# Quarter slots for short last tiles of experts, and columns of A moved on chip, in a graph layer followed by a mixture of experts

## The chip, the cores and the metric

One core of a Trainium2 chip runs the whole program. The engines have instruction streams of their own: TensorE (PE, with its weight loads shown as PEld), VectorE (DVE), ScalarE (ACT), GpSimd (POOL) and SyncE (SP), which issues most DMAs. The metric is the device time of one launch in microseconds. Everything is float32 unless said otherwise.

## The reference

```python
edge_index = jnp.stack([src, dst])                       # 67584 edges, sorted by dst
x = x + gnn(layernorm(x), edge_weight, edge_index, node_vec1)
x = x + moe_ffn(layernorm(x)[None], Wr, br, ln_g, ln_b, W1, b1, W2, b2)[0]

# gnn:  segment_sum(w[:, None] * xn[dst], src, 2048) + node_vec1
# moe:  logits = xt @ Wr + br; the best 2 of 8 experts; weights renormalised
#       xn = layernorm(xt); xe = xn * ln_g[e] + ln_b[e]
#       y = gelu(xe @ W1[e] + b1[e], exact) @ W2[e] + b2[e]
```

x is 2048 x 256; an expert has 256 inputs and 1024 hidden units. So 4096 (token, expert) rows are computed. With the reference's own inputs the eight experts get 544, 509, 506, 482, 502, 510, 536 and 507 rows (counted by running the reference's routing).

## The kernel before

**Graph stage.** The sparse sum is made dense: A (2048 x 2048) is built in 32 steps of 64 columns (`for n in range(NH)`), two steps to a block `cb` of 128 columns. In step n DVE and POOL make the one-hots `hl` and `hr` of step n+1 (`make_hots`, three buffers each, lines 306 to 318). PE multiplies them in `make_cols` (line 343): 96 bf16 products with a stationary operand of 32 columns, at four column positions of the array by turns (`tile_position=(0, j * RK)`), each 128 wide. ACT copies each half of the result to `ar` (line 346; three buffers). The row of `ar` is (column in a group of four, block of A's rows), which is not how PE needs it, so SP writes `ar` to DRAM (`ad`, line 347) and, once a block's two steps are there, loads it back with a column of A to each partition (`ac`, line 350). `dense` (line 357) then multiplies, for two blocks of output rows, the `ac` tiles of a group of three or four blocks by `xn_sb`, the normalised x with 8 router columns (264 wide); `add` (lines 364 to 369) adds that to `acc` on DVE. These 40 pieces of work (`todo`) are dealt out by a budget: from step 8 on each step earns 3.5, a piece of a group costs its number of blocks (3 or 4), and the last step runs what is left of all groups but the last. On PE a step's pieces come after its `make_cols`, and PE works strictly in that order. Tiles `ac` come from two pools of four buffers, used by the groups in turn; a block of group g takes a buffer of group g-2. `xn_sb` is written by ACT in steps 0 to 3 (line 519), its router columns by DVE in step 5 (line 515). If some edge fell outside the windows, a branch after the stage does the sum another way; it isn't taken here.

**Expert stage.** Rows are routed on chip. A whole slot has 256 rows of one expert, a half slot 128. `run_slot` does the first layer (`layer_1`, line 1013: 8 chunks of the hidden units, two 256-wide products of two instructions each, the gelu on ACT at line 1015), the turning and scaling of the next slot's rows (`head`, lines 978 to 1002), and the second layer (`layer_2`, line 1027, twice for a whole slot), after which POOL adds rows to `y_d` in DRAM by index (`put_y`, line 1035). PE's order is written out by hand (`manual_schedule`). `slots` (lines 858 to 909) counts on DVE each expert's tiles: `n_of[:, 0]` whole slots and `n_of[:, 1]` a half slot for an odd tile; from it come the expert numbers `slot_i`, read into registers of SP (line 1134), and the row lists. The third expert's rows (`whole[3]`) are the first that need these. Ten whole slots always run (`FIRST = 10`, of which the loop at line 1151 runs u = 3 to 9); more run under nested conditions (line 1162), then the halves (line 1169), and at the end two whole slots (`final`) whose results are written to `out` after `y_d` has been copied there (line 1180). Weights and rows of the first two half slots are loaded in u = 4 and 5, and half 0's `head` runs in u = 8.

With the counts above, 34 tiles of 128 rows are needed: 16 whole slots (10, then 4, then the 2 at the end) and 2 half slots.

Of the kernel before, what the change touches and what calls it, by code (L numbers as in the profile page):

```python
# [9 lines left out]
F32 = mybir.dt.float32  # L10
BF16 = mybir.dt.bfloat16
F16 = mybir.dt.float16
I32 = mybir.dt.int32
# [13 lines left out]
def kernel(  # L27
# [57 lines left out]

    consts = ctx.enter_context(tc.tile_pool(name="consts", bufs=1))
# [60 lines left out]
    slot_i = consts.tile([1, NU + 2], I32, name="slot_i")  # L147
    xr_d = dram.tile([N + TS, RW], F32, name="xr_d")
    y_d = dram.tile([N + TS, D], F32, name="y_d")
    cols_d = dram.tile([NE, P, KH + 2 * KD], F32, name="cols_d")  # L150
# [178 lines left out]
    def make_cols(n, hl, hr):  # L329


        cb, h = n // 2, n % 2
        if h == 0:
            ads[cb] = dram.tile([P, NB, P], F32, name="ad", bufs=4)
        ad_v = ads[cb].rearrange("(m j) b r -> (j b) m r", m=GB // QP)
        ar = rowsp.tile([P, GH // QP, P], F32, name="ar")
        for m0 in range(0, GH // QP, 4):
            pa = ps_a.tile([P, 4, P], F32, name="pa")
            for m in range(4):
                for i in range(3):  # L340
                    for j in range(QP):
                        g = (m0 + m) * QP + j
                        nc.tensor.matmul(pa[j * RK:(j + 1) * RK, m, :], hr[:, i, g, :],  # L343
                                         hl[:, g, :], start=(i == 0), stop=(i == 2),
                                         tile_position=(0, j * RK))
            nc.scalar.copy(ar[:, m0:m0 + 4, :], pa)  # L346
        nc.sync.dma_start(ad_v[:, h * GH // QP:(h + 1) * GH // QP, :], ar)
        if h == 1:
            acs[cb] = pool_of[cb].tile([P, NB, P], F32, name="ac")
            nc.sync.dma_start(acs[cb], ads[cb])  # L350
# [20 lines left out]
    ads, acs = {}, {}  # L371
    ET = mybir.EngineType
    ALL = {ET.DVE, ET.Pool, ET.PE, ET.Activation, ET.SP}
    with tc.manual_schedule(engines=ALL):
# [88 lines left out]
        for n in range(NH):  # L463
# [36 lines left out]
            if n >= 8:  # L500
                budget += 3.5
# [8 lines left out]
            if n < 2:  # L510
                weigh_x(2 + n)
            elif n == 2:
                nc.scalar.copy(acc[:, :, D:], xl.rearrange("p (b e) -> p b e", e=NE))
            elif n == 5:
                nc.vector.tensor_tensor(xn_sb[:, :, D:], acc[:, :, D:],
                                        rs[:, :, None].to_broadcast([P, NB, NE]), OP.mult)
            if n < 4:
                for b in range(4 * n, 4 * n + 4):
                    nc.scalar.activation(xn_sb[:, b, :D], acc[:, b, :D], AF.Identity,
                                         bias=shift[:, b:b + 1], scale=rs[:, b:b + 1])  # L520
            if n == 1:
# [47 lines left out]
    with tc.If(n_used < E):  # L569
        nc.sync.dma_start(xn_d.rearrange("(b p) d -> p b d", p=P), xn_sb)  # L570
# [72 lines left out]
    class Slot:  # L643


        def __init__(self, i, n, set_, to, head_, early=False):
# [5 lines left out]

    LAST = 2
# [4 lines left out]
             for i, k in enumerate(numbers)]  # L658
    final = [Slot(FIRST - EARLY, TT, 3, AHEAD + 2, 2), Slot(FIRST - EARLY + 1, TT, 6, AHEAD + 6, 0)]
    halves = [Slot(NF + i, 1, 4 + i if i < 2 else i % 3, AHEAD + 3 + i % 3, 3 + i % 2)  # L660
              for i in range(NE)]
    with tc.manual_schedule(engines=ALL - {ET.Pool}):
# [195 lines left out]
        def slots(ps):  # L858


            small_t = lambda name, dt=F32: route.tile([P, NE], dt, name=name, bufs=1)
            flag = flags[:, 1:1 + NE]
            tiles_i = small_t("tiles_i", I32)
            nc.vector.tensor_tensor(tiles_i, ps, over, OP.add)
            nc.vector.tensor_scalar(tiles_i, tiles_i, 7, None, op0=OP.arith_shift_right)
# [9 lines left out]
                                           op1=OP.subtract)  # L875
            upto = route.tile([P, 2, NE], F32, name="upto", bufs=1)
# [20 lines left out]
            nc.vector.tensor_copy(slot_i[:, NU:], upto[0:1, :, NE - 1])  # L897
# [69 lines left out]
        def load_slot(s):  # L967
            load_weights(s)
            load_rows(s)
# [89 lines left out]
        def run_slot(s, nxt, more=(), between={}, put=put_y):  # L1059
            for m in more:  # L1060
                m()
            hT = layer_1(s)
            if nxt is not None:
                head(nxt)
            layer_2(s, hT, put, between)

        def later(load, *slots):
            return [lambda s=s: load(s) for s in slots]
# [68 lines left out]
        )  # L1137
        load_slot(whole[EARLY])
# [10 lines left out]
        for t in so_far:  # L1149
            nc.vector.memset(t, 0.0)  # L1150
        for u in range(3, FIRST):
            more = later(load_slot if u + 2 <= FIRST else load_rows, whole[u + 2])
            more += later(load_slot, *{4: halves[:1], 5: halves[1:2], 7: final[:1], 8: final[1:]}.get(u, []))
            also = {FIRST - 2: halves[0], FIRST - 1: final[0]}.get(u)
            run_slot(whole[u], whole[u + 1], more, {1: lambda: head(also)} if also else {})
# [3 lines left out]
    )  # L1159
    with ExitStack() as nest:  # L1160
# [6 lines left out]
    with ExitStack() as nest:  # L1167
        for u, s in enumerate(halves):
            nest.enter_context(tc.If(n_half > s.i - NF))
            with tc.manual_schedule(engines=ALL - {ET.Pool}):  # L1170
                if u >= 2:
                    head(s)
                run_slot(s, halves[1] if u == 0 else None,
                         later(load_slot, *halves[u + 1:u + 2] * (u > 0)))
# [38 lines left out]
```

## Time and profile before

| what | us |
|---|---|
| three timed runs | 505.18, 511.9, 511.95 (median 511.9) |
| the profiled execution | 508.05 |
| its span, first to last instruction | 506.3 |
| mean granted TensorE clock | 0.945 of full |

In the profile, a line like `PE L343 MATMUL pa<-hl,hr ... x96` is a run of 96 instructions of line 343, with its start and length; a bracket after it gives the engine's idle time before it and what ended that. The chain of waits follows the work that ended last backwards; an entry there is a start, a length and what took it.

### The profile page before, as it was taken

How to read it: one execution, taken by the hardware profiler on the slowest of the kernel's cores; microseconds unless marked ns; L12 is line 12 of the kernel's file. 1: busy time of each engine (PE TensorE's matmuls, PEld its weight loads, DVE VectorE, ACT ScalarE, POOL GpSimd, SP SyncE). 2: the span in 40 equal slices, each digit the busy share in tenths (PEclk: the TensorE clock that was granted, in tenths of full speed). 3: DMA queues.
4: the chain of work that ended last, by engine and by line, in shares of the span. 5: the costliest groups of instructions: out<-in, count | busy, mean ns of one | idle time of the engine just before them, and what ended most of it. 6: DMA issues, size and time to landing. Idle time of an engine off the chain costs nothing.

```text
span 506.3 us, 12113 instructions
## 1 busy us (share of the span) xinstructions
PE 459.8 (91%) x4996; PEld 394.4 (78%) x4996; DVE 273.1 (54%) x621; ACT 183.8 (36%) x422; POOL 192.7 (38%) x158
## 2 busy tenths in 40 slices
PE   4876599898979999899999899999999999999993
PEld 3775478687758878788888788888888888888882
DVE  7999999999969971317837232323232312212111
ACT  2478524144214210028483323332243433333320
POOL 3477655544533330000142444443452444322231
PEclk9575679899979999999999999999999999999998
DMA  6128678796777667953513997997999677226420
GB/s 214 53 76 246 203 223 269 230 236 186 203 216 221 210 178 239 344 189 105 179 54 84 303 333 214 361 356 210 334 360 309 169 210 210 36 40 204 140 92 31
DMA packets 84356, 102.15 MB, mean 202 GB/s; under 512 B 8240, under 2 KB 74656, under 8 KB 82176
## 3 DMA queue, kind: packets, MB, share of 16 engines
q1 hardware_dynamic: 74832, 86.26, 53.5%
q0 software_dynamic: 7984, 13.91, 11.9%
q10 hardware_dynamic: 1472, 1.06, 0.7%
q8 instruction: 44, 0.72, 0.6%
q14 instruction: 24, 0.20, 0.1%
HBM read 75.18 MB, written 28.14 MB: 204 GB/s over the span
## 4 chain that ended last, share of the span: by engine, by line
PE 35%; DMA 13%; issue 3%; DVE 1%; SPq 0%; ACT 0%; POOL 0%; POOLq 0%; DVEq 0%
PE py L1027 16%; PE ph L1013 15%; DMA xs<-xr_d,to_i 8%; DMA y_d<-ys,to_i 2%; DMA out<-y_d 2%; PE px L978 1%; PE px L834 1%; PE py L357 1%; DMA so_far<-out,to_i 1%; DMA out<-ys,to_i 0%; SPq L1180 0%; POOL out L1048 0%; POOLq L1209 0%; ACT L1015 0%; DVE pick L957 0%
## 5 line engine op out<-in xcount | busy, mean ns | idle before, releaser
L357 PE MATMUL py<-xn_sb,ac 128*128 128x264 f32 x512 | 126.3, 404 | 1.8 <-DVEq L569 1.4
L1013 PE MATMUL ph<-xeT,w 128*128 128x256 f32 (+1 forms) x576 | 121.3, 368 | 2.4 <-PEq L1167 1.7
L1027 PE MATMUL py<-w,hT 128*128 128x256 f32 x544 | 121.0, 379 | 0.0
L1013 PEld LDWEIGHTS ph<-xeT,w 128*128 128x128 f32 x576 | 104.4, 190 | 16.5 <-issue 3.0
L357 PEld LDWEIGHTS py<-xn_sb,ac 128*128 128x128 f32 x512 | 98.5, 197 | 21.7 <-issue 2.2
L1027 PEld LDWEIGHTS py<-w,hT 128*128 128x128 f32 x544 | 101.9, 190 | 12.9
L1015 ACT ACTIVATE hT<-ph,ec 128x256 f32<-128x256 f32 (+1 forms) x144 | 66.2, 462 | 117.6 <-PE ph L1013 60.8
L1035 POOL DMA_INDIRECT y_d<-ys,to_i x30 | 48.5, 1616 | 119.3 <-DVE ys L1030 88.5
L318 POOL TENSOR_TENSOR hr<-eq,w 128x1024 bf16<-128x1024 bf16 x32 | 61.2, 1912 | 81.6 <-DVE hr L318 66.1
L343 PE MATMUL pa<-hl,hr 128*32 128x128 bf16 x3072 | 58.4, 237 | 21.6 <-POOL hr L318 10.8
L343 PEld LDWEIGHTS <-hr 128*32 128x32 bf16 x3072 | 50.0, 106 | 32.6 <-issue 14.0
L306 DVE TENSOR_TENSOR hl<-k,iota_t 128x4096 bf16<-128x4096 bf16 x32 | 72.9, 2278 | 0.0
L987 DVE TENSOR_SCALAR xeT<-px,ec 128x256 f32<-128x256 f32 (+1 forms) x38 | 18.4, 526 | 79.8 <-PE px L978 79.0
L939 POOL DMA_INDIRECT xs<-xr_d,to_i x39 | 40.5, 1038 | 54.2 <-DVE z L702 41.9
L346 ACT COPY ar<-pa 128x512 f32<-128x512 f32 x64 | 36.5, 584 | 59.8 <-PE pa L343 53.6
L1030 DVE SCALAR_TENSOR_TENSOR ys<-py,wt,b2w 128x256 f32<-128x256 f32 x34 | 16.4, 484 | 72.7 <-PE py L1027 61.3
L364 DVE TENSOR_TENSOR acc<-acc,py 128x528 f32<-128x528 f32 x32 | 22.3, 701 | 35.3 <-PE py L357 35.3
L318 DVE TENSOR_TENSOR hr<-eq,w 128x2048 bf16<-128x2048 bf16 x32 | 39.1, 1223 | 0.6
L1002 ACT ACTIVATE b2w<-b,wt 128x256 f32<-128x256 f32 x36 | 16.3, 500 | 34.0 <-DVE wt L1000 32.4
L311 DVE TENSOR_TENSOR eq<-k,iota_t 128x1024 bf16<-128x1024 bf16 x32 | 21.8, 680 | 0.0
L670 ACT ACTIVATE sq<-acc,less_m 128x256 f32<-128x256 f32 x16 | 8.0, 499 | 32.6 <-DVE acc L364 32.6
L296 ACT CAST w<-r 128x256 bf16<-128x256 f32 x16 | 6.5, 405 | 25.0 <-DVE r L295 25.0
(196 smaller groups left out, 303.0 us busy)
## 6 DMA issues: line engine op xcount, KB each, us to landing
w<-in_L_ffn_W SPq DMA_DIRECT2D x40, 1024.0 KB, 9.2
ad<-ar SPq DMA_DIRECT2D x32, 512.0 KB, 8.7
ac<-ad SPq DMA_DIRECT2D x16, 1024.0 KB, 5.9
b<-in_L_ffn_b SPq DMA_DIRECT2D x20, 128.0 KB, 9.8
out<-y_d SPq DMA_DIRECT2D x4, 512.0 KB, 6.3
xr_d<-rec SPq DMA_DIRECT2D x1, 1300.0 KB
y_d<-acc SPq DMA_DIRECT2D x1, 1280.0 KB, 5.1
acc<-in_x SPq DMA_DIRECT2D x2, 512.0 KB, 7.6
```

What stands on the lines that cost most here:

```text
L306: nc.vector.tensor_tensor(hl.rearrange("p g (n t) -> p g n t", t=2), two(k2[:, 0], g, P), pair(P), OP.is_equal)
L311: nc.vector.tensor_tensor(eq.rearrange("p g (n t) -> p g n t", t=2), two(k2[:, 1], g, RK), pair(RK), OP.is_equal)
L318: return engine.tensor_tensor(hr[:, i0:i1].rearrange("p i g (n t) -> p (i g) n t", t=2), eq[:, None, :, :].to_broadcast([P, i1 - i0, GH, RK]),
L343: nc.tensor.matmul(pa[j * RK:(j + 1) * RK, m, :], hr[:, i, g, :], hl[:, g, :], start=(i == 0), stop=(i == 2), tile_position=(0, j * RK))
L346: nc.scalar.copy(ar[:, m0:m0 + 4, :], pa)
L357: nc.tensor.matmul(pa[:, i, :DX], acs[c][:, b + i, :], xn_sb[:, c, :], start=(c == cbs[0]), stop=(c == cbs[-1]))
L364: nc.vector.tensor_add(acc[:, b:b + 2, :], acc[:, b:b + 2, :], pa[:, :, :DX])
L939: nc.gpsimd.indirect_dma_start(out=(sets[s.set][0] if into is None else into)[:, t, :], out_offset=None, in_=(xr_d if rows is None else ro ...
L1013: nc.tensor.matmul(ph, w1[:, k, c * P:(c + 1) * P], xeT[:, k, :], start=(k == 0), stop=(k == KD - 1))
L1015: nc.scalar.activation(hT[:, c, :s.n * P], ph, AF.Gelu, bias=ec[:, c:c + 1], scale=1.0)
L1027: nc.tensor.matmul(py, hT[:, c, t * P:(t + 1) * P], w2[:, c, :], start=(c == 0), stop=(c == KH - 1))
L1035: st = nc.gpsimd.indirect_dma_start(out=y_d[:, :], out_offset=bass.IndirectOffsetOnAxis(ap=tos[s.to][:, t:t + 1], axis=0), in_=ys, in_offs ...
```

## The change

**Columns of A.** `ar` no longer goes through DRAM. As soon as ACT has copied half of a step's result, four DMAs of 64 KB move its four 128 x 128 pieces straight to `ac`, each to eight partitions that are four apart; of a step's eight, six are issued by SP and two by ACT. So `ac` is allocated at a block's first step. The columns of a block now stand in another order in the partitions, so `xn_sb` has to be permuted likewise: at the end of step 3 four DMAs write it to DRAM (`xn_p`) in permuted rows, and in step 5 one DMA reads all of it back in place. Its router columns are therefore written in step 3, and pieces of `dense` begin in step 7.

**Quarter slots.** An expert whose odd tile has 1 to 32 rows gets a quarter slot in place of a half slot, for at most two experts (`NQ`). `slots` finds them (`few_e`, `few_t`) and takes them out of the halves. Both quarter slots always run, spread over u = 7 to 9: the rows are the stationary operand (32 columns), four products at four column positions make the hidden units as 32 rows x 4 x 256, which are turned by two transposes, and the second layer leaves four partial sums that one product with `fold` adds up. The halves come ahead of the conditional whole slots, and load their data when they run.

```diff
+    xn_p = dram.tile([P, NB * DX], F32, name="xn_p")
+    xp = xn_p.rearrange("(q j m) f -> q m j f", m=4, j=8)
...
         if h == 0:
-            ads[cb] = dram.tile([P, NB, P], F32, name="ad", bufs=4)
-        ad_v = ads[cb].rearrange("(m j) b r -> (j b) m r", m=GB // QP)
+            acs[cb] = pool_of[cb].tile([P, NB, P], F32, name="ac")
...
             nc.scalar.copy(ar[:, m0:m0 + 4, :], pa)
-        nc.sync.dma_start(ad_v[:, h * GH // QP:(h + 1) * GH // QP, :], ar)
-        if h == 1:
-            acs[cb] = pool_of[cb].tile([P, NB, P], F32, name="ac")
-            nc.sync.dma_start(acs[cb], ads[cb])
+            for m in range(m0, m0 + 4):
+                c = h * P // 2 + m0 * QP * GC + m % 4
+                queue = nc.sync if m < 6 else nc.scalar
+                queue.dma_start(acs[cb][c:c + 4 * QP * GC - 3:4], ar[:, m, :])
...
-            if n >= 8:
+            if n >= 7:
                 budget += 3.5
...
-            elif n == 5:
+            elif n == 3:
                 nc.vector.tensor_tensor(xn_sb[:, :, D:], acc[:, :, D:],
                                         rs[:, :, None].to_broadcast([P, NB, NE]), OP.mult)
+            elif n == 5:
+                nc.sync.dma_start(xn_sb.rearrange("p b d -> p (b d)"), xn_p)
...
+            if n == 3:
+                for i in range(4):
+                    nc.sync.dma_start(xp[i], xn_sb[32 * i:32 * (i + 1)])
...
+            few_i = small_t("few_i", I32)
+            nc.vector.tensor_scalar(few_i, tiles_i, QR.bit_length() - 1, None,
+                                    op0=OP.arith_shift_right)
+            nc.vector.tensor_scalar(few_i, few_i, TS // QR - 1, None, op0=OP.bitwise_and)
...
+            nc.vector.tensor_scalar(is_few, few_i, float(P // QR), None, op0=OP.is_equal)
+            n_few = small_t("n_few")
+            nc.vector.tensor_tensor_scan(n_few, ones[:, :NE], is_few, 0.0, op0=OP.mult, op1=OP.add)
+            last = small_t("last")
+            nc.vector.scalar_tensor_tensor(last, iota_p[:, :NE], float(NB), tiles[:, :NE],
+                                           op0=OP.mult, op1=OP.add)
+            for i in range(NQ):
+                it = small_t(f"few{i}")
+                nc.vector.scalar_tensor_tensor(it, n_few, float(i + 1), is_few, op0=OP.is_equal,
+                                               op1=OP.mult)
+                nc.vector.tensor_sub(n_of[:, 1, :], n_of[:, 1, :], it)
+                of_it = small_t(f"of_few{i}")
+                for t, v in ((few_e, iota_p[:, :NE]), (few_t, last)):
+                    nc.vector.scalar_tensor_tensor(of_it, it, 1.0, v, op0=OP.mult, op1=OP.mult,
+                                                   accum_out=t[:, i:i + 1])
+            nc.vector.tensor_scalar(few_t, few_t, -1.0, None, op0=OP.add)
+            nc.vector.tensor_copy(slot_i[:, NU + 2:], few_e[0:1, :])
...
+            def first():
+                ph = ps_h.tile([P, TS], F32, name="ph")
+                for k in range(KD):
+                    for j in range(QW):
+                        nc.tensor.matmul(ph[part(j), :], xeT[:, k, :],
+                                         w1[:, k, j * TS:(j + 1) * TS], start=(k == 0),
+                                         stop=(k == KD - 1), tile_position=(0, j * QR))
+                nc.vector.tensor_copy(hs, ph)
...
+            def second():
+                pa = listed.rearrange("p a b -> p (a b)")
+                for t in range(TT):
+                    for j in range(QW):
+                        nc.tensor.matmul(pa[part(j), :], hT[:, t, part(j)], w2[:, j * TT + t, :],
+                                         start=(t == 0), stop=(t == TT - 1),
+                                         tile_position=(0, j * QR))
+                nc.vector.tensor_copy(py, pa)
+
+            def total():
+                pa = counts.rearrange("p a b e -> p (a b e)")[:QR, :D]
+                nc.tensor.matmul(pa, fold, py, start=True, stop=True)
...
+            if 0 <= f - 1 < NQ:
+                between_1 = {1: ready[1], 5: ready[2]}
+                between[0] = ready[3]
+                between.setdefault(1, lambda: None)
+                t0, t1 = between[1], ready[4]
+                between[1] = lambda t0=t0, t1=t1: (t1(), t0())
```

Here f is u - 7; `between_1` names the chunks of a whole slot's first layer ahead of which a step of the quarter slot stands (the products of `first` ahead of chunk 1, the transposes of `turn_h` ahead of chunk 5), and `between` the halves of its second layer ahead of which `second` (0) and `total` (1) stand.

## The prediction

> **What bounds the kernel now.** I read the page's busy slices first, then busy time by stage (cut where PE's lines change), then the chain of waits, and the timeline around what the change touches. Busy tenths in 40 slices of 12.7 us:
>
> ```profile
> PE   4876599898979999899999899999999999999993
> DVE  7999999999969971317837232323232312212111
> ```
>
> DVE fills the first third, PE everything after. The stages (columns: PE, PEld, DVE, ACT, POOL busy, granted clock, DMA share, GB/s):
>
> ```profile
> 66.30:191.70 125.40, 116.10 (x2542) 93.99 (x2534) 112.14 (x142) 39.26 (x91) 55.49 (x35) 0.95 0.75 218
> 191.70:238.50 46.80, 45.28 (x222) 38.13 (x211) 16.34 (x37) 13.48 (x41) 0.52 (x3) 1.00 0.68 226
> 238.50:452.40 213.90, 211.86 (x1041) 185.84 (x1039) 74.90 (x295) 79.72 (x169) 83.15 (x65) 1.00 0.73 222
> 452.40:469.20 16.80, 14.59 (x99) 13.38 (x99) 3.26 (x12) 6.39 (x17) 4.32 (x4) 1.00 0.63 167
> 469.20:506.30 37.10, 28.30 (x132) 24.64 (x132) 4.68 (x11) 8.48 (x18) 9.69 (x9) 0.94 0.28 90
> ```
>
> From the first `dense` (66.3) to the last `make_cols` (191.7) PE idles 9.3 us of 125 and DVE 13.3: both bind by turns. Then PE alone binds. From 238.5 to 452.4 (whole slots) it idles 2.0 us; 452.4 to 469.2 is the two half slots; the last row is the two final slots and the writes. The chain agrees:
>
> ```profile
> 268.87 0.67 PE listed L813 x12
> ...
> 280.14 7.48 DMA xs<-xr_d,to_i
> 287.63 0.04 issue
> 287.67 0.44 PE px L978 x2
> ...
> 309.27 6.91 PE ph L1013 x32
> ```
>
> PE's one wait among the slots is at 287.67, for the third expert's rows, gathered after `slots`. 32 instructions of 256 columns take 6.91 us, 0.216 each. In the graph stage:
>
> ```profile
> 47.40 2.08 ACT L519 ACTIVATE xn_sb<-acc,shift,rs 128x256 f32<-128x256 f32 x4
> ...
> 108.94 1.52 PE L343 MATMUL pa<-hl,hr 128*32 128x128 bf16 x96
> 110.39 2.94 PE L357 MATMUL py<-xn_sb,ac 128*128 128x264 f32 x12
> ```
>
> `xn_sb` is complete at 49.5. The 96 products with 32 columns take 1.45 us up to the next line, 15 ns each; the 12 full ones of L813, of the same 128 columns and width of data, 56 ns each: four column positions overlap 3.7-fold in 16-bit.
>
> **Half slots out.** PE's 14.6 busy us of 452.4 to 469.2 go, and half 0's head (0.22). The 2.2 us of PE idle there stand at the two exits from nested conditions ("PEq L1160" 0.6, "PEq L1167" 1.7); two exits remain, one now after u = 9, so they stay. The end behind follows PE as before: the last scatter is now a whole slot's second, 0.9 us after that slot's PE work at 453.3, against 469.1 for the last half's with `final` starting at 469.2. Gain 14.8.
>
> **Quarter slots in.** PE executes, for each: `turn` 0.22 (as half a head), `first` and `second` 16 instructions of 256 columns each, `turn_h` 0.22, `total` 0.43. In series `first` is 16 x 0.216 = 3.46; at the 3.7-fold overlap 0.93. Bounds: 2 x 2.7 = 5.5 us and 2 x 7.8 = 15.6. A written f32 product is two instructions (the page counts 544 of L1027 for 272 written), and both go to the same 32 columns, so only the second of one can lie beside the first of the next: 2-fold, 1.9 with the ends. So 4.7 each, 9.4 in all. [...] The DVE copies, the bias and the gelu between these steps have three to four chunks of 0.86 us on PE as cover; DVE is 35% busy in this stage. If that cover fails, each quarter slot adds the 0.5 us of a copy. Loads are unchanged (two slots' weights in u = 4 and 5); POOL scatters two of 32 rows; `fold` is one small DVE instruction in u = 3, under the same cover.
>
> **More in `slots`.** 15 DVE instructions and four accumulator reads, at the 0.18 us from start to start of its 28 neighbours between 268.28 and 273.30, and 0.1: 3.1 us. Behind them on DVE stand the new row lists, the scaling of slot 2's rows and `ys`; for them waits POOL's gather, and for that PE at 287.67. It is later by all of it, as PE waits already: +3.1, at least 0 (if the gather's 7.5 us shrink) and at most 3.4 with two more register loads.
>
> Expert stage: -14.8 + 9.4 + 3.1 = -2.3, from -9.3 to +4.2.
>
> **Columns on chip.** Behind `ar` stood two DMAs:
>
> ```profile
> ad<-ar SPq DMA_DIRECT2D x32, 512.0 KB, 8.7
> ac<-ad SPq DMA_DIRECT2D x16, 1024.0 KB, 5.9
> ...
> y_d<-acc SPq DMA_DIRECT2D x1, 1280.0 KB, 5.1
> ```
>
> 48 become 256 of 64 KB. At 0.34 to 0.43 us of queue time per issue, SP's six cost 2.4 of a step's 5.4 us (125.4 over 23 steps; SP has little else there), ACT's two 0.8 of its 3.7 us idle. PE waited 0.4 us in all for `ac`, so the shorter path itself gives nothing. The router columns' product (0.28 us on DVE) only moves from step 5 to 3. ACT's DMAs can wait for an `ac` buffer; I walked the budget: block 7 (step 14) needs group 0 done, now at step 13; block 10 (step 20) waits one piece, 2.9 us; block 13 (step 26) until step 27, about 7 us with ACT's copies queued behind. Three PSUM buffers cover that, or nearly: 0 to 1.
>
> **One step earlier.** By the budget, 28 pieces instead of 26 are done before step 31, so two of the six behind it (72 instructions, 16.3 us with their adds) go from there: -5.9, PE alone binding. They must fit before, where PE idles 9.3 us, 6.6 of it "issue" stalls of which I can't say that they give way. I take half as absorbed: -3.
>
> **`xn_sb` through DRAM.** 2112 KB are written after 49.5, and read back only then: SP waits in between, with the columns of step 6 on queued behind it, and step 7's `dense` waits on PE with every later `make_cols` behind. At y_d's pace (1280 KB in 5.1 us) the write takes 8.4; reading at ac's pace (1024 KB in 5.9) at most 12.2, I take 9 as half of the 5.9 is not bytes. 49.5 + 0.8 of issue + 17.4 = 67.7 (range 62 to 71): first `dense` 1.4 us later than now, though one piece ahead, and DVE, three buffers ahead, runs on. I count this in the absorbed half. Graph stage: -3, from -5.9 to +2.
>
> [...]
>
> **The sum.** -2.3 - 3 = -5.3: span 501, execution 502.8 from the profiled 508.05. That lies 3.9 under the median 511.9 (runs 505.18 to 511.95), so I go up by a third of it: 504.
>
> **Rivals.** *The detour of `xn_sb` is the new wait* (slower). If the four writes keep a quarter of the engines busy, then at 343 GB/s for 0.98 of 16 engines (200 to 210 us), 21.9 KB/us each, 2.16 MB take 24.7 us, ready at 84. PE idles from about 63 and is 18 behind, DVE stops when its three buffers are full at about 74; the idle time behind recovers 6 or so. Graph stage +11, with -2.3: +9, 518. It decides from a write of about 14 us on. For it: 32 partitions a DMA, where every row above has 128. Against: four DMAs in flight at once. *No overlap in f32*: quarter slots 15.6, +0.9 in all, 510. For: the pairs of instructions. *Full overlap*: 5.5, and -5 in the graph stage: -11, 498. For: the 3.7-fold of L343. *The slots don't apply*: 544 rows leave exactly 32, the limit, and 536 leave 24; a row more and one half stays, +7.3, 511. The nearest routing choice is decided by 0.0003 of a logit, so unlikely.
>
> **Chances.** Forecast 0.36, full overlap 0.18, detour 0.33, no overlap 0.11, not applied 0.02. Range 496 to 519, 2 us past full overlap and 1 past the detour; some 0.2 lies outside. 2%, about what a measurement here can tell from no change, is 10 us. Faster by that: full overlap and a third of the forecast's spread, 0.3; slower: four fifths of the detour, 0.27; within, 0.43.
>
> **What would show it.** Right: first `dense` near 67, no PE gap there, 48 instructions of L357 behind step 31, `first` at about 1.9 us, rows of slot 3 some 3 us later after `slots`, no half slots after u = 13. Wrong: PE idle between 63 and 84 with the read of `xn_p` issued near 75 (detour); `first` near 3.5 or 0.95; ACT waiting for `ac` in other steps than 20 and 26, or column DMAs that land later than 5.4 us each step, which would make DMA the bound.

## The result, and the profile after

| kernel | median us | runs | ratio [95%] |
|---|---|---|---|
| before | 508.86 | 505.18 to 511.95, 4 runs | |
| changed | 543.4 | 542.05 to 546.87, 4 runs | 1.069 [1.058, 1.080] |

The change makes the kernel 34.5 us slower; the range forecast ended at 519. The profiled execution of the changed kernel took 546.87, its span is 544.8; that is 38.5 more than the span in the profile of before, and this execution is the slowest of the four. Busy tenths in 40 slices, now of 13.6 us each:

```profile
PE   4877510398999998798999989999999969999993
DVE  7986920099999999322485733222333321222111
```

PE and DVE stand still together in the sixth to eighth slice, some 35 us; before, DVE had no such hole. The time line of PE (start, length, engine and line, work; in brackets the idle time before it and what ended that) shows where:

```profile
66.92 2.75 PE L351 MATMUL pa<-hl,hr 128*32 128x128 bf16 x96 [2.63 <-ACT ar L354]
103.98 4.50 PE L367 MATMUL py<-xn_sb,ac 128*128 128x264 f32 x12 [34.30 <-DMA ac<-ar]
```

L367 is `dense`: its first instruction comes at 103.98, and came at 66.35 before. The releaser named, `ac<-ar`, is only the wait that ended last of several; SP's own time line shows what else stands ahead:

```profile
55.27 8.29 SPq L360 DMA_DIRECT2D ac<-ar  x8
63.67 5.30 SPq L536 DMA_DIRECT2D xn_p<-xn_sb  x4
69.07 24.65 SPq L360 DMA_DIRECT2D ac<-ar  x12
93.83 0.49 SPq L528 DMA_DIRECT2D xn_sb<-xn_p  x1
```

The four writes of `xn_sb` are issued from 63.67 on, then the twelve column DMAs of steps 4 and 5, which take SP 24.65 us in place of some 8, and only then the read. What the DMA engines did meanwhile (the first two rows of the DMA view for 64 to 104 us: mean busy tenths of the 16 engines and GB/s in 40 slices of 1 us):

```profile
DMA  5422543353224222222232212233335959999321
GB/s 158 165 101 84 167 134 123 129 202 137 104 104 151 109 104 96 112 104 121 106 136 122 70 53 85 58 85 102 96 98 159 309 221 407 424 373 407 128 78 49
```

From 66 to 94 two or three tenths of the engines are busy in most slices and some 110 GB/s move, the columns included; in the read, behind 94, it is up to nine tenths and about 400 GB/s. The write can be told from the columns by its packets, 128 of 16.9 KB: in the trace they run from 65.3 to 87.5, four at a time. Meanwhile the columns hardly move: of their 512-byte packets on SP's queue 3 start between 74 and 84. SP, which waits for earlier column transfers before it issues more, stands still for 32.2 us in all (its waits between 40 and 110 us: total, times, longest):

```profile
SPq L360 <- DMA ac<-ar: 32.2, 8, 9.9
```

So when the write has landed at 87.5, eight columns are still to be issued ahead of the read, which follows 6.3 us later.

The stages, in the columns of the table of before (from the last products ahead of the gap to the first `dense`; to the last `make_cols`; what is left of `dense`; row choosing and slots up to u = 9; the jump over the halves with what surrounds it; the two final slots):

```profile
66.90:104.00 37.10, 2.77 (x97) 2.53 (x96) 5.25 (x4) 4.25 (x12) 6.21 (x5) 0.55 0.43 150
104.00:234.70 130.70, 122.05 (x2654) 99.15 (x2654) 113.69 (x145) 39.44 (x92) 52.99 (x33) 0.97 0.40 110
234.70:276.90 42.20, 40.06 (x195) 33.70 (x188) 15.19 (x35) 13.55 (x42) 0.52 (x3) 1.00 0.64 213
276.90:435.00 158.10, 154.27 (x805) 131.14 (x805) 63.88 (x266) 60.41 (x128) 59.44 (x47) 1.00 0.77 240
435.00:452.00 17.00, 12.45 (x49) 9.47 (x49) 4.77 (x18) 2.76 (x6) 5.68 (x6) 0.90 0.62 168
507.00:544.80 37.80, 28.30 (x132) 24.63 (x132) 5.08 (x12) 8.50 (x18) 9.82 (x9) 0.95 0.30 90
```

From the first to the last `dense` the two kernels take the same: 172.4 us before (66.35 to 238.72, where the row choosing starts), 173.0 now (103.98 to 276.95). Only the cut between the second and third row moved: 130.7 and 42.2 us in place of 125.4 and 46.8, since fewer pieces are left for the end. The DMA share fell from 0.75 to 0.40, and that brought nothing. From the last `dense` to the end of the span it is 267.6 before and 267.9 now, although the half slots are gone. Two places in it answer for that. The quarter slots themselves are cheap, and a jump isn't (PE's time line, in u = 7 and at u = 10):

```profile
407.37 1.07 PE L1151 MATMUL ph<-w,xeT 128*32 128x256 f32 x16
408.37 3.72 PE L1056 MATMUL ph<-xeT,w 128*128 128x256 f32 x16
...
444.02 0.67 PE L1056 MATMUL ph<-xeT,w 128*128 128x256 f32 x2 [0.97 <-PEq L1312]
448.27 8.43 PE L1056 MATMUL ph<-xeT,w 128*128 128x256 f32 x30 [3.58 <-issue]
```

`first` (L1151) is 16 instructions in 1.00 us up to the next line, 62 ns each against 216 ns for one that uses all columns of the array: 3.5-fold overlap in f32 (216 / 62). But at the eleventh whole slot, where the code of eight half slots is jumped, PE loses 0.97 and 3.58 us and runs 30 instructions in 8.43 in place of 6.5: 6.5 us in all.

So the loss is one stretch of 37.6 us in the graph stage, which the stage behind doesn't give back, and a gain in the expert stage that another place takes away. The experiments ask whether the stretch is the trip of `xn_sb` through DRAM (theory 1) or the 256 column transfers (theory 2), and what each other part is worth.

### The profile page after: what moved, and what is told of

It reads as the page before. It is cut to its first block, busy times and chain, and to the rows that moved or that the text cites. A ratio compares the mean times of both kernels' runs of the same rounds, so it can differ in the third digit from the quotient of the medians.

```text
span 544.8 us, 12426 instructions
## 1 busy us (share of the span) xinstructions
PE 458.9 (84%) x4972; PEld 387.5 (71%) x4972; DVE 276.3 (51%) x643; ACT 178.8 (33%) x408; POOL 191.0 (35%) x157
## 5 line engine op out<-in xcount | busy, mean ns | idle before, releaser
L367 PE MATMUL py<-xn_sb,ac 128*128 128x264 f32 x512 | 123.7, 397 | 36.6 <-DMA ac<-ar 34.5
L367 PEld LDWEIGHTS py<-xn_sb,ac 128*128 128x128 f32 x512 | 96.1, 193 | 56.5 <-issue 37.4
L1056 PE MATMUL ph<-xeT,w 128*128 128x256 f32 x512 | 116.9, 385 | 5.6 <-issue 3.6
L1070 PE MATMUL py<-w,hT 128*128 128x256 f32 x512 | 114.3, 380 | 0.0
L1056 PEld LDWEIGHTS ph<-xeT,w 128*128 128x128 f32 x512 | 97.6, 192 | 21.6 <-issue 5.7
L1070 PEld LDWEIGHTS py<-w,hT 128*128 128x128 f32 x512 | 95.8, 190 | 13.1 <-issue 0.8
L1058 ACT ACTIVATE hT<-ph,ec 128x256 f32<-128x256 f32 x128 | 60.5, 474 | 110.1 <-PE ph L1056 59.2
L1078 POOL DMA_INDIRECT y_d<-ys,to_i x28 | 45.4, 1623 | 108.0 <-DVE ys L1073 73.8
L351 PE MATMUL pa<-hl,hr 128*32 128x128 bf16 x3072 | 62.0, 239 | 22.7 <-ACT ar L354 8.5
L351 PEld LDWEIGHTS <-hr 128*32 128x32 bf16 x3072 | 53.0, 106 | 34.6 <-issue 23.4
L982 POOL DMA_INDIRECT xs<-xr_d,to_i x36 | 37.6, 1044 | 57.7 <-DVE z L721 40.9
L1030 DVE TENSOR_SCALAR xeT<-px,ec 128x256 f32<-128x256 f32 x34 | 16.9, 539 | 75.1 <-PE px L1021 74.4
L377 DVE SCALAR_TENSOR_TENSOR acc<-py,cols,acc 128x256 f32<-128x256 f32 x16 | 7.0, 478 | 36.4 <-PE py L367 36.3
```

The costliest lines, as they stand in the source:

```text
L367: nc.tensor.matmul(pa[:, i, :DX], acs[c][:, b + i, :], xn_sb[:, c, :], start=(c == cbs[0]), stop=(c == cbs[-1]))
L982: nc.gpsimd.indirect_dma_start(out=(sets[s.set][0] if into is None else into)[:, t, :], out_offset=None, in_=(xr_d if rows is None else ro ...
L1056: nc.tensor.matmul(ph, w1[:, k, c * P:(c + 1) * P], xeT[:, k, :], start=(k == 0), stop=(k == KD - 1))
L1058: nc.scalar.activation(hT[:, c, :s.n * P], ph, AF.Gelu, bias=ec[:, c:c + 1], scale=1.0)
L1070: nc.tensor.matmul(py, hT[:, c, t * P:(t + 1) * P], w2[:, c, :], start=(c == 0), stop=(c == KH - 1))
L1078: st = nc.gpsimd.indirect_dma_start(out=y_d[:, :], out_offset=bass.IndirectOffsetOnAxis(ap=tos[s.to][:, t:t + 1], axis=0), in_=ys, in_offs ...
```

## The experiments

Each ratio is to runs of the kernel before on the same chip (medians 504.4 to 508.9); times in brackets are of kernels whose experts get other numbers of rows. "First" is the start of the first `dense`, "end" the start of the row choosing behind the last one, "rest" what is left of the span from there.

| run | median us | ratio [95%] | first | end | first to end | rest |
|---|---|---|---|---|---|---|
| before, profile shown | 508.86 | | 66.35 | 238.72 | 172.4 | 267.6 |
| before_again | 510.24, one run | | 66.89 | 242.29 | 175.4 | 266.2 |
| the change | 543.4 | 1.069 [1.058, 1.080] | 103.98 | 276.95 | 173.0 | 267.9 |
| change_again | 547.08, one run | | 103.19 | 276.96 | 173.8 | 268.0 |
| quarter_only | 508.98 | 1.006 [1.002, 1.011] | 66.84 | 242.82 | 176.0 | 262.2 |
| quarter_only_again | 510.4, one run | | 66.77 | 244.51 | 177.7 | 264.1 |
| quarter_halves_last | 517.79 | 1.026 [1.018, 1.033] | 68.09 | 244.08 | 176.0 | 272.1 |
| cols_only | 542.49, one run | | 102.73 | 274.47 | 171.7 | 266.2 |
| no_detour | (558.04) | | 69.19 | 242.93 | 173.7 | |
| straight_write | (571.87) | | 86.70 | 257.78 | 171.1 | |
| cols_neighbours | 566.28 | 1.117 [1.109, 1.125] | 77.52 | 302.64 | 225.1 | 263.0 |
| cols_neighbours_sp | 517.38 | 1.019 [1.009, 1.028] | 66.91 | 251.59 | 184.7 | 261.6 |
| moved_by_pe | 522.26 | 1.032 [1.027, 1.038] | 85.22 | 257.74 | 172.5 | 262.4 |
| moved_by_pe_71 | 528.05 | 1.043 [1.037, 1.049] | 83.42 | 263.65 | 180.2 | 262.9 |
| moved_by_pe_5ar | 539.1 | 1.067 [1.061, 1.073] | 83.85 | 273.64 | 189.8 | 262.7 |
| x_twice | 513.59 | 1.019 [1.014, 1.023] | 76.56 | 247.87 | 171.3 | 263.1 |
| before_7 | 507.5 | 1.007 [1.002, 1.012] | 61.61 | 237.81 | 176.2 | 267.9 |
| quarter_7 | 506.24 | 1.002 [0.998, 1.006] | 64.22 | 244.29 | 180.1 | 260.7 |

**The two halves of the change apart.** `cols_only` is the kernel before with the graph hunks of the diff, `quarter_only` the change without them:

```diff
-            for m in range(m0, m0 + 4):
-                c = h * P // 2 + m0 * QP * GC + m % 4
-                queue = nc.sync if m < 6 else nc.scalar
-                queue.dma_start(acs[cb][c:c + 4 * QP * GC - 3:4], ar[:, m, :])
+        nc.sync.dma_start(ad_v[:, h * GH // QP:(h + 1) * GH // QP, :], ar)
+        if h == 1:
+            acs[cb] = pool_of[cb].tile([P, NB, P], F32, name="ac")
+            nc.sync.dma_start(acs[cb], ads[cb])
...
-                for i in range(4):
-                    nc.sync.dma_start(xp[i], xn_sb[32 * i:32 * (i + 1)])
```

> The kernel before with the graph part of the change alone (columns moved on chip, xn_sb permuted through DRAM, pieces from step 7). Theory (the graph part makes the whole loss): first dense at 104 us, the last one ends at 277, 544 to 548 in all. Rival (graph and expert parts act on one another): an end of the last dense that differs from 277 by over 4 us.

> The change without its graph part: columns of A go through DRAM as before, pieces of dense begin in step 8, xn_sb is not permuted; the quarter slots and the halves ahead of the whole slots stay. Theory (the graph part makes the whole loss): first dense at 66 us and end of the last dense at 239, as before; the expert stage as in the change (267.7 us from there to the end, against 267.4 before), so within 1 % of the kernel before, 505 to 511. Rival (the expert part costs as well, for instance through later weights or through the end of the graph stage): slower than before by 5 us or more. In both the skip of the eight half slots ahead of the eleventh whole slot is expected to cost PE about 6.5 us, as it did in the change.

`cols_only` took 542.49 with its first `dense` at 102.73: the graph part alone makes the whole loss. `quarter_only` is at 1.006 of before. Its rest of 262.2 is 5.4 us shorter than before's, and the jump at the eleventh whole slot, expected to cost 6.5, cost 0.89 (its PE time line):

```profile
410.26 7.14 PE L1045 MATMUL ph<-xeT,w 128*128 128x256 f32 x32 [0.89 <-PEq L1301]
```

**The place of the half slots.**

```diff
     with ExitStack() as nest:
+        for u in range(FIRST, len(whole)):
+            nest.enter_context(tc.If(n_whole > whole[u].i))
...
+    with ExitStack() as nest:
         for u, s in enumerate(halves):
             nest.enter_context(tc.If(n_half > s.i - NF))
```

> As quarter_only, but the nested conditions of the half slots stand behind those of the whole slots again, as before. Theory (the 6.5 us that PE lost at the eleventh whole slot come from jumping the code of eight half slots just ahead of a slot that would otherwise follow without a gap): no gap at the eleventh slot, the exit before the last two slots costs some 2 us as in the kernel before, and the run is 4 to 7 us faster than quarter_only and than before, 498 to 504. Rival (the price belongs to the jump and moves with it): the gap of about 6 us appears ahead of the last two slots, and the time stays within 2 us of quarter_only.

Neither: the run is 8.8 us slower than `quarter_only`. The gap moved to the last two slots, as the rival said, but grew (PE's time line of this run):

```profile
476.38 10.15 PE L1045 MATMUL ph<-xeT,w 128*128 128x256 f32 x32 [8.61 <-PEq L1308]
```

8.61 us of idle time and 3.1 more in the 32 instructions behind it (7.07 elsewhere), 11.7 in all, for two jumps one behind the other.

**What of the change varies by itself.**

> The changed kernel unaltered, for what its stages vary by: first dense is expected at 102 to 106 and the last dense to end at 274 to 280. If the 6.5 us that PE lost at the eleventh whole slot belong to the program, they come again within 1 us; if they hang on what the DMA engines do at that moment, any loss from 1 to 10 us.

First `dense` at 103.19, end at 276.96. At the eleventh whole slot PE lost 1.11 and 2.87 us and 2.5 in the 30 instructions behind, 6.5 again. So this loss seems to belong to the program as it was built; `quarter_only`, with the same expert code and the same jump, lost 0.89 and in its second profile 1.12. What sets it (where the landing lies in the code, how the instructions are loaded) wasn't tried and stays open. The trace gives a lead and no answer: blocks of 16 KB of instructions start to load at 445.9 and 449.4 in the changed kernel, in and behind the idle time, but one does at 411.2 in `quarter_only` too, just behind its jump, and nothing is lost there.

**Without the trip of `xn_sb`.**

```diff
-            elif n == 5:
-                nc.sync.dma_start(xn_sb.rearrange("p b d -> p (b d)"), xn_p)
...
-            if n == 3:
-                for i in range(4):
-                    nc.sync.dma_start(xp[i], xn_sb[32 * i:32 * (i + 1)])
```

> The change without the permutation of xn_sb: neither the four writes to xn_p nor the read; the product then pairs columns of A with wrong rows of xn_sb, and as the router sees other values, the experts get other numbers of rows, so only the graph stage is to be read. Theory 1 (the detour holds the first dense): PE goes from step 7's products straight to dense at 70 to 76 us, and the last dense ends at 240 to 250. [...]

PE's time line of `no_detour`:

```profile
66.72 2.53 PE L351 MATMUL pa<-hl,hr 128*32 128x128 bf16 x96 [2.79 <-DVE eq L320]
69.19 1.75 PE L367 MATMUL py<-xn_sb,ac 128*128 128x264 f32 x4
74.65 3.86 PE L367 MATMUL py<-xn_sb,ac 128*128 128x264 f32 x8 [3.71 <-DMA ac<-ar]
```

The gap of 34 us is gone, the end is at 242.93: theory 1. Of theory 2 a small part is left, the 3.71 us for columns behind the first `dense`.

**The trip with a straight write.**

```diff
-                for i in range(4):
-                    nc.sync.dma_start(xp[i], xn_sb[32 * i:32 * (i + 1)])
+                nc.sync.dma_start(xn_p, xn_sb.rearrange("p b d -> p (b d)"))
```

> The change with xn_sb written to xn_p by one DMA of 128 partitions in straight order in place of four of 32 partitions in permuted rows; the read stays where it is. The permutation is left out by that, so the router sees other values and only the graph stage is to be read. Theory (the four writes are slow because each ran on four engines, 24 us for 2.1 MB): the one write uses all engines and takes 7 to 10 us, the read is issued at 73 to 78, first dense at 80 to 88. Rival (the trip through DRAM costs that in whatever form, by its bytes or behind the columns on SP): first dense still after 95.

SP's time line of this run, and then PE's:

```profile
63.41 0.39 SPq L535 DMA_DIRECT2D xn_p<-xn_sb  x1
64.97 12.29 SPq L360 DMA_DIRECT2D ac<-ar  x12
77.31 0.45 SPq L528 DMA_DIRECT2D xn_sb<-xn_p  x1
```

```profile
86.70 5.51 PE L367 MATMUL py<-xn_sb,ac 128*128 128x264 f32 x12 [17.19 <-DMA xn_sb<-xn_p]
```

The same bytes in the same place, in one DMA of 128 partitions: the read is issued at 77.3 in place of 93.8 and PE starts at 86.70. SP's DMA queue in 6 us of each write (packets, MB, and their time as a share of 16 engines), first the four writes (76 to 82 in the changed kernel), then the one (65 to 71 here):

```profile
q1 hardware_dynamic: 40, 0.57, 22.3%
```

```profile
q1 hardware_dynamic: 265, 2.06, 90.5%
```

34 of the first 40 packets are the write's and 118 of the other 265; the rest are small. 22.3% is the time of 3.6 engines, 90.5% that of 14.5. The one write's 128 packets run from 64.5 to 71.3, up to sixteen or seventeen at a time: 6.8 us in place of 22.3, at the same 0.63 us for the median packet. This run changes the number of DMAs, the partitions of each and the order of the rows in DRAM together; which of them makes it four at a time, no run separates, and as the traces don't number the engines, they don't show on which ones each of the four writes ran.

So the 37.6 us divide: 103.98 - 86.70 = 17.3 for the form of the four writes; 86.70 - 69.19 = 17.5 for the rest of the trip, of which 9.4 runs from the read's issue and 8.1 lies ahead of it, while SP issues the columns of steps 4 and 5 that stand behind the write; and 69.19 - 66.35 = 2.8 for the columns on chip. This last one sets a kernel that begins `dense` in step 7 against one that begins in step 8; against `before_7` below, which begins in step 7 too, it is 7.6, and 5.1 at the end (242.93 and 237.81), in single profiles of which two of the same kernel differed by up to 3.6.

**Columns to neighbouring partitions.** The permutation is only needed because a piece goes to partitions four apart. Eight neighbours keep the natural order:

```diff
-                c = h * P // 2 + m0 * QP * GC + m % 4
-                queue.dma_start(acs[cb][c:c + 4 * QP * GC - 3:4], ar[:, m, :])
+                c = h * P // 2 + m * QP * GC
+                queue.dma_start(acs[cb][c:c + QP * GC], ar[:, m, :])
```

> The change with each 128 x 128 piece of ar moved to eight neighbouring partitions of ac in place of eight that are four apart: the columns then stand in their natural order, so neither the permutation of xn_sb nor its trip through DRAM is needed, and its router columns are scaled in step 5 again. Theory 1 (the trip was the loss): first dense at 64 to 75, last dense ends at 234 to 244, 497 to 508 in all. Theory 2 (the 256 column transfers are a price of their own, and neighbours make it worse): PE waits for ac in many steps and the last dense ends after 250, over 515 in all.

> As cols_neighbours, with all eight transfers of a step issued by SP. If ACT's 2.7 us per step for its two transfers (1.3 of issue, 1.4 idle) hold up the first steps: first dense 2 to 5 us earlier than in cols_neighbours. If SP's issue time binds (8 x 0.61 = 4.9 us of a step's 5.4, more in the first steps): PE waits for ac in most steps, and the last dense ends over 4 us later than in cols_neighbours. If neither counts: within 1 % of it.

Theory 2 holds here: with neighbours the transfers are the bound. The two rows below are the DMA view of `no_detour` (four apart) and of `cols_neighbours_sp` (neighbours) for 100 to 160 us: packets, MB, and the time of the packets as a share of 16 engines.

```profile
q1 hardware_dynamic: 11921, 5.30, 32.5%
```

```profile
q1 hardware_dynamic: 12808, 5.72, 51.4%
```

8% more bytes took 58% more engine time; the median 512-byte packet of the whole stage took 27 ns four apart and 44 as neighbours. With two of eight transfers on ACT, ACT waited 102.0 us for `ac<-ar` in 22 places between 28 and 300 us, and 11.4 us of that reach PE at once ("11.43 <-ACT ar" ahead of step 7). With all on SP it is 59.0 us, the first `dense` comes at 66.91, but SP issues back to back (its time line):

```profile
30.67 53.19 SPq L358 DMA_DIRECT2D ac<-ar  x72
```

53.19 / 72 = 0.74 us each, eight to a step 5.9, while a step took 5.4 before. PE then waits 6.8 us in one place at 215 to 222, near the end of the graph stage. Taking the transfers from ACT helps, by more than was expected (10.6 us at the first `dense`, 49 in all). The signs named for a bound by SP did not come: PE waits for `ac` twice, 4.7 us in all, and the last `dense` ends 51 us earlier than in `cols_neighbours`. That SP's issuing makes the 184.7 us from first to end is argued from its time line alone.

**The permutation on PE.** 16 products of x with a permutation matrix, out of which ACT scales with permuted `rs` and `shift`; the branch not taken moves `xn_sb` back through DRAM:

```diff
+                    if b % 2 == 0:
+                        pt = ps_s.tile([P, 2, 512], F32, name="py1")
+                    nc.tensor.matmul(pt[:, b % 2, :D], perm, acc[:, b, :D], start=True, stop=True)
-                    nc.scalar.activation(xn_sb[:, b, :D], acc[:, b, :D], AF.Identity,
-                                         bias=shift[:, b:b + 1], scale=rs[:, b:b + 1])
+                    nc.scalar.activation(xn_sb[:, b, :D], pt[:, b % 2, :D], AF.Identity,
+                                         bias=both_p[:, 1, b:b + 1], scale=both_p[:, 0, b:b + 1])
```

`moved_by_pe_71` has `m < 7` for `m < 6` (one transfer on ACT), `moved_by_pe_5ar` has five buffers of `ar` for three.

> The change with xn_sb permuted on PE and not through DRAM: in steps 0 to 3 each block of x is multiplied by a permutation matrix (16 products of 256 columns, some 7 us of PE in all) and ACT scales it out of PSUM with permuted rs and shift; the router columns follow in step 6 by one product more. Columns stay four partitions apart, six of a step's eight transfers on SP and two on ACT. Theory 1 (the trip through DRAM and the wait of DVE for the router columns were the graph stage's loss; what is left is ACT's 2.7 us a step and SP's issue time): first dense at 67 to 76, last dense ends at 234 to 243, 497 to 505 in all. Theory 2 (the 256 transfers and their queue time cost by themselves): PE waits for ac or ar by over 10 us between 66 and 240, last dense ends after 247, over 508 in all.

> As moved_by_pe, with seven of a step's eight transfers on SP and one on ACT. If ACT's time in its transfers holds up the first steps: first dense 1 to 4 us earlier, total 0 to 3 us less than moved_by_pe. If SP binds (7 x 0.66 = 4.6 us of a step's 5.4, and it ran back to back at 8): the columns run late, PE waits for ac, 2 us or more slower.

> As moved_by_pe, with five buffers of ar in place of three, so that ACT can copy two steps further ahead of the column transfers. If ACT's waits for ar's transfers hold up the hots' consumers: ACT's wait for ac<-ar falls from tens of us to under 10, total 1 to 4 us less. If SP's queue sets the pace: the waits go to SP and the time stays within 1 %.

The first `dense` comes at 83 to 85 in all three, not at 67 to 76. Waits of `moved_by_pe` between 28 and 250 us (who waited for what: total, times, longest):

```profile
DVE hl L320 <- PE pa L356: 17.0, 3, 6.9
...
ACT xn_sb L550 <- PE py L549: 13.7, 14, 2.0
...
PE py L549 <- ACT xn_sb L550: 9.5, 8, 3.5
```

PE and ACT wait for one another at each pair of blocks, with all later work of both behind, until even DVE runs out of buffers for 17.0 us; in the profile before, DVE waited for nothing between 28 and 66. From the first `dense` on it takes 172.5 again. Seven transfers on SP made that 180.2, five buffers of `ar` 189.8: ACT's wait for `ac<-ar` did fall, from 27.7 to 14.6, but PE waited 14.6 for it; why the columns came later was not taken apart. So theory 1 fails at the start. Theory 2 has the end (257.74) and the total right, but not their cause: between 66 and 240 PE waits 4.2 us for `ac` and `ar`, not over 10.

**x loaded twice.** 16 DMAs at the start bring x straight into permuted partitions of `xn_sb`; the products of `moved_by_pe` fall away:

```diff
+            nc.sync.dma_start(xn_sb[c:c + 29:4, :, :D], xq[q, m])
...
-                    nc.scalar.activation(xn_sb[:, b, :D], pt[:, b % 2, :D], AF.Identity,
+                    nc.scalar.activation(xn_sb[:, b, :D], xn_sb[:, b, :D], AF.Identity,
```

> As moved_by_pe, but with no products of x and no work on the path of the first steps: x is loaded a second time, at the start, by 16 DMAs on SP straight into permuted partitions of xn_sb, and ACT scales it in place with permuted rs and shift (one small product) in steps 0 to 3; the router columns follow in step 6 by one product. Theory (the total follows the moment of the first dense, as every form of the columns took 172 to 174 us from there to the end of the last one): first dense at 66 to 72, the last ends at 239 to 246, 497 to 507 in all. Rival (the 256 transfers hold the start by themselves, since ACT pays 2.7 us a step for its two): first dense after 76, over 510 in all.

1.019 of before, the first `dense` at 76.56 and the total of 513.59: both lie in the rival's range, the first by half a microsecond. PE's time line shows the first steps held by ACT and by columns (three of the lines between 48 and 81):

```profile
48.00 0.37 PE L562 MATMUL pa<-ident,b_rows 64*128 64x64 f32 x1 [6.90 <-ACT ar L364]
...
76.56 1.16 PE L377 MATMUL py<-xn_sb,ac 128*128 128x264 f32 x4 [2.19 <-DMA ac<-ar]
80.86 3.86 PE L377 MATMUL py<-xn_sb,ac 128*128 128x264 f32 x8 [3.15 <-DMA ac<-ar]
```

From there it takes 171.3. But this run has a delay of its own, which its rival leaves out. SP's time line:

```profile
7.55 32.28 SPq L120 DMA_DIRECT2D xn_sb<-in_x  x16
39.95 50.38 SPq L370 DMA_DIRECT2D ac<-ar  x46
```

The 16 loads of x hold SP until 39.83, so its first column transfer is issued at 39.95, and at 30.66 in the change; ACT starts to scale x at 44.38, behind a wait of 7.3 us. How much of the 10 us ahead is this, how much ACT's column transfers, and how much the small product that `rs` and `shift` pass through, the run doesn't tell. It doesn't show that the 256 transfers hold the start by themselves.

**One step earlier, alone.**

```diff
-            if n >= 8:
+            if n >= 7:
```

> The kernel before with one part of the change alone: pieces of dense begin in step 7. The prediction's term: 28 pieces in place of 26 are done ahead of the last step, worth -5.9 us, of which it took half as absorbed (-3). If it is right: 24 instructions of dense fewer behind the last make_cols (88 less of them in place of 112 after the stage's end on SP, ACT and POOL or 48 in place of 72 ahead of it), the last dense ends at 233 to 240, the total 1 to 6 us less. If the first steps are bound by DVE and all of it is absorbed: the extra piece only makes PE wait for the columns of step 5 in step 7, the end moves by less than 2 us, the total within 0.5 %.

> quarter_only with pieces of dense from step 7, as a candidate: quarter slots (262 to 264 us from the last dense to the end, against 266 to 267 before) and columns through DRAM. If the term of one step earlier is worth what the prediction took: 500 to 505 and faster than before. If it is absorbed: 505 to 511, as quarter_only.

`before_7` is at 1.007 [1.002, 1.012]. Its first `dense` comes 4.7 us earlier and then PE waits (its time line):

```profile
61.61 2.13 PE L357 MATMUL py<-xn_sb,ac 128*128 128x264 f32 x4
69.37 3.89 PE L357 MATMUL py<-xn_sb,ac 128*128 128x264 f32 x8 [5.63 <-DMA ac<-ad]
```

The columns of step 5 aren't there sooner, so the step is absorbed by 5.63 us of PE waiting. `quarter_7` is at 1.002 [0.998, 1.006], no measurable difference. No version tried beats the kernel before.

**What the stages vary by.**

> The kernel before unaltered, for what its stages vary by: the last dense ended at 238.7 in the profile shown, with 6.6 us of issue stalls among the products of make_cols. If these stalls are chance, the end moves by 3 us or more either way here; if they belong to the program, it stays within 1 us. The expert stage is expected at 267.4.

> quarter_only unaltered, for what its stages vary by. If its later end of the graph stage (242.9 against 238.7) was chance, it lies between 235 and 241 here at one of two looks; if the changed program itself is slower there, at 242 to 246 again. The expert stage from there to the end is expected at 262 in both.

The kernel before ended its graph stage at 238.72 and at 242.29 in two executions; its issue stalls of PE among `make_cols` were 6.6 and 7.3 us. The four profiles with quarter slots and columns through DRAM ended it at 242.8, 244.5, 244.1 and 244.3, the three without (`before_7` with them) at 238.7, 242.3 and 237.8; the stalls, from the first `dense` on, were 10.5, 8.2, 8.5 and 7.9 us in the four, 6.6, 7.3 and 3.7 in the three. So some 4 us of what the quarter slots gain behind (rest 262.3 on average, without `quarter_halves_last`, against 267.2) are lost ahead of it, in a stage whose code they don't touch. That leans towards the program and not chance, but the ranges nearly meet, and the cause stays open.

## Why the prediction was wrong

**The detour of `xn_sb`** was the failed step: the forecast counted it in the absorbed half, at a first `dense` 1.4 us later, and it cost 34.8 (103.98 - 69.19). The forecast had `xn_sb` back at 67.7; the first `dense` came at 103.98. "49.5 + 0.8 of issue + 17.4" goes wrong at the start, in the write and ahead of the read; only the read itself took about what was forecast:

| term | forecast | measured |
|---|---|---|
| write issued | 49.5 | 63.67 |
| write takes | 8.4 | 23.9, from issue to its last packet's end at 87.5 |
| read issued | with the write's end | 93.83, 6.3 behind it |
| read takes | 9 | 10.2 to the first `dense` |

The start is late because the row it was read from belongs to the kernel before. In the change ACT finishes `xn_sb` at 56.4, since its two transfers a step keep it from other work for 1.4 us, 1.3 of it the issuing, priced at 0.8; and SP has the columns of step 3 to issue first. The write took what the rival said (24.7): four packets at a time. As one DMA of 128 partitions it took 6.8 from first packet to last, under the 8.4 of the forecast, so the pace was right for a write that keeps 14.5 of the 16 engines in use; the four writes kept 3.6. The read had to wait for the columns besides, as SP issued it only behind the twelve of steps 4 and 5 (69.07 to 93.72).

That the four writes shared the same four engines is an estimate from these counts and from the four packets at a time, against sixteen of the one; no run shows what sets the number.

**The rival named the mechanism and missed its size**: ready at 84 and +11 in the graph stage, against 103.98 and +38. Its 49.5 and its missing queue were the forecast's. Above all it had "the idle time behind recovers 6 or so": seven rows of the table with the columns on chip show 171 to 174 us from first to end, with PE starting anywhere from 69 to 104, so a late start was paid to within some 3 us. (The rows that depart from this, with 180 to 225, have other transfers or buffers.) DVE had stopped too, for 36.3 us, at its first sum of what `dense` gives (L377), so neither of the two engines that bind by turns had work done ahead to give back; that this is the reason is argued, not tested.

**Columns on chip, "0 to 1".** The transfers were priced at the 0.34 to 0.43 us of the old, large ones. Each took 0.61 on SP, 256 in place of 48, and without the trip the first `dense` came 2.8 us later than before (7.6 later than in `before_7`, which begins in step 7 too), with 3.7 us of waiting for columns behind it. That the router columns' product "only moves from step 5 to 3" was wrong as well: in step 3 DVE waits 4.4 us for the copy by ACT that it reads. That lies ahead of the first `dense`, where DVE waited for nothing in the profile of before.

**One step earlier, "half as absorbed".** Alone it brings nothing that can be measured (`before_7`).

**Quarter slots, 9.4 at two-fold overlap.** No run shows the two-fold overlap, which was the author's estimate. The products overlap 3.5-fold: `first` took 1.00 us where 1.9 was forecast. The steps of one slot are 0.23, 1.00, 0.22, 1.00 and 0.55 us: 3.0 and not 4.7, 6.0 for two, near the rival of full overlap (5.5). The argument from pairs fails: that two instructions of one f32 product go to the same columns did not hold the overlap to two.

**More in `slots`, +3.1.** PE waited 1.95 and 1.37 us for the rows in place of 1.88: +1.4.

**"Two exits remain", so their idle time stays.** In the change as built the exit that was moved ahead costs 6.5 us, in `quarter_only` 0.9. With these terms the expert stage's sum would be -14.8 + 6.0 + 1.4 = -7.4. With the costly jump it came to 267.9 against 267.6; where the jump was cheap, to 262.3 against 267.2 on average, which is -4.9. The 2.5 us between were not traced.

Of the signs named ahead two came: "PE idle between 63 and 84 with the read of `xn_p` issued near 75", 20 and 19 us later (it ends at 103.98, the read is issued at 93.83), and `first` near 0.95 (1.00).

## What to carry to other kernels

Ask of every new DMA what pattern it has on both sides (the same bytes took 22.3 us in four writes here and 6.8 in one) and what stands ahead of it on its queue (twelve columns and 24.65 us ahead of the read), and start its clock from the changed kernel's order, not from the old trace. Where two engines bind by turns through a few buffers, as here, a late start may be paid nearly in full (37.6 us late at the first `dense`, 38.2 at the end of the last one): look hardest at a trip that must be over before the main loop begins. A transfer that the loop hides gave nothing here when it got shorter, and 256 small ones in place of 48, at 0.61 us each on SP, cost the issuing engines time that reached PE in the first steps (3.71 us of waiting behind the first `dense` of `no_detour`).

## What was not expected of the hardware

- Eight destination partitions four apart and eight neighbours are not the same to a DMA: 27 and 44 ns for the median 512-byte packet (`no_detour` and `cols_neighbours_sp`), 32.5% of the engines for 5.30 MB and 51.4% for 5.72. No run here varied the distance further.
- One f32 product of 32 columns at each of four column positions: 16 instructions in 1.00 us, 62 ns each against 216.
- A jump over the same code cost PE 0.9 to 1.1 us in one program, 6.5 in another (twice the same there), and two jumps in a row 11.7.
- In the first steps of the changed kernel ACT does no other work for 1.36 to 1.47 us at most pairs of transfers that it issues ("1.37 <-issue" ahead of its work at 54.36); 1.29 to 1.40 of that is the issuing (53.03 to 54.32 there), so the 2.7 us a step of the expectations count one stretch twice.
- Four writes in flight together ran four packets at a time for 18.1 of their 22.3 us and hardly ever more, and the column transfers queued with them came almost to a stop (3 of their 512-byte packets started on SP's queue in 10 us).
